# A graph network with two attentions on one core: the sixteen largest of a row of scores found through fourteen groups, and a new loop order

## Chip, core and metric

The program runs on one core of a Trainium2 chip. The metric is the device time of one execution in microseconds. Engines: PE (matmuls and transposes), DVE (vector engine), ACT (activations and copies), POOL (GpSimd), SP (issues the DMAs). Each engine works off its own instructions in order.

## The reference

Two rounds of a graph layer and an attention over 1250 nodes with 512 features. The change lies in the last part, the second attention, with 8 heads of 64 features. For every node and head it keeps the 16 largest of the 1250 scores and takes the softmax over these alone:

```python
logits = jnp.einsum('bmd,bpd->bmp', qd * scale, kd)
_, idx = lax.top_k(logits, TOPK)            # TOPK = 16
k_sel = gather(k, idx)
v_sel = gather(v, idx)
attn = jax.nn.softmax(jnp.einsum('bmd,bmkd->bmk', q * scale, k_sel), axis=-1)
out = jnp.einsum('bmk,bmkd->bmd', attn, v_sel)
...
return out @ wo_w.T + wo_b
```

The result is added to the features that went in.

## The kernel before

The nodes are cut into T = 10 tiles of P = 125 rows; the features into K = 4 pieces of 128. The stages run one after the other: adjacency counts, first graph layer, first attention, eight experts, second graph layer, projections, second attention. A general path for other inputs (`tile_general`) follows under a condition and runs only if the flag `bad` was set at the end.

The second attention is a hand-written order of instructions (`tc.manual_schedule`). It has 40 steps n; step n stands for the row tile i = n // 4 and a pair of heads j = n % 4; a_ = 0, 1 names the head of the pair. One turn of the loop mixes three steps: scores and selection of step n, transposes of step n - 1, products with the values of step n - 2. The helpers, with the engine that each keeps busy:

- `scores1` (PE, L1592): scores of one head in PSUM, a tile S of 3 x 512 columns of which 1250 are used, made in three chunks of two matmuls. There is one S for each a_, so the next scores of the same a_ wait until the last reader, the sign, is through.
- `first1` (DVE, L1606): the eight largest of the row; on POOL the negated maximum `nm` (L1607) and `gap` (L1608, L1609), a tiny distance that keeps the sixteenth itself inside the threshold.
- `without1` (DVE, L1617): a copy of the row, `rest`, in which these eight are replaced by a very low number.
- `second1` (DVE, L1626): the eight largest of `rest`; on POOL `below` (L1627), the negated threshold.
- `weights1` (ACT, L1634): e = exp(score - maximum) for all 1250 columns.
- `select1` (ACT, L1641): sg = sign(score + below), summed into `signs`; then on POOL e = e * sg (L1644). Columns outside the sixteen become negative.
- `turn1` (PE, L1654) and `keep1` (ACT, L1661): five groups of four transposes of e through one PSUM bank; ACT copies each group out with a Relu, which drops the negative columns. A group waits until the copy of the group before has emptied the bank.
- `values1` (PE, L1710) and `outputs1` (ACT, L1720): the product with the values. `project1` (PE, L1728) and `finish1` (DVE, L1736; DMA L1738): output projection, a quarter of the columns in each step, added to X and sent.
- `sums1`, `sums_exp1`, `sums_over1`, `sums_wide1`, `sums_turn1`, `sums_keep1`, `scale1`: once in four steps the sums of the sixteen weights of all heads, their inverses, and the scaling of the output (POOL L1670, L1684, L1698; ACT L1673, L1695; DVE L1677, L1678; PE L1691).
- `halves1`: in two of four steps the queries of the next row tile are split into a high and a low half (ACT L1577, POOL L1578) and copied to the other partitions by DMA (L1579, L1580).
- `signs_over1`, after the loop: if for any row the count in `signs` isn't that of sixteen columns, `bad` is set.

Lines used in the prediction from other stages: L644 (normalisation, DVE), L1383 (bias to X, POOL), L1530 (bias to X, DVE), L1091 (row maximum in the first attention, DVE, from PSUM), L776 (adjacency banks copied by ACT in transposed order, a stride of ten columns), L638 and L1421 (one-column operations on DVE).

Of the kernel before, what the change touches and what calls it, by code (L numbers as in the profile page):

```python
# [20 lines left out]
P = 125  # L21
# [551 lines left out]
def tile_usual(ctx: ExitStack, tc: tile.TileContext, a: dict, out: bass.AP):  # L573
# [969 lines left out]

    TINY = 2.0 ** -22
    wo_pool, wo_p = pool("wo", 1)
# [4 lines left out]
    with (  # L1550
# [6 lines left out]
        ps_s1 = (ps_s1a, ps_s1b)  # L1557
        w_v = at1.tile([128, K, D], F32, name="w_v1b", bufs=1)
# [4 lines left out]
        score, found, bests, es, pTs, outs, turned = {}, {}, {}, {}, {}, {}, {}  # L1563
# [18 lines left out]
        def scores1(n, a_, *chunks):  # L1582
# [6 lines left out]
            for c in chunks:  # L1589
                n0, n1 = c * 512, min(c * 512 + 512, N)  # L1590
                for x in range(2):
                    nc.tensor.matmul(score[n, a_][:, n0:n1], stacks[i][:, x, h, :], K2[:, h, n0:n1],  # L1592
                                     start=(x == 0), stop=(x == 1))


        def first1(n, a_):
            if n > last:
                return
# [5 lines left out]
            nm = at1.tile([P, 1], F32, tag=f"nm{a_}", name="nm1")  # L1604
            gap = at1.tile([P, 1], F32, tag=f"gap{a_}", name="gap")
            nc.vector.max(out=top[:, 0:8], in_=score[n, a_][:, :N])  # L1606
            nc.gpsimd.tensor_scalar(nm, top[:, 0:1], -1.0, None, op0=ALU.mult)  # L1607
            nc.gpsimd.tensor_scalar(gap, top[:, 7:8], -1.0, top[:, 0:1], op0=ALU.mult, op1=ALU.max)  # L1608
            nc.gpsimd.tensor_scalar(gap, gap, TINY, None, op0=ALU.mult)  # L1609
            found[n, a_] = (nm, gap, top)  # L1610

        def without1(n, a_):
            if n > last:
                return
            nm, gap, top = found[n, a_]
            rest = at1.tile([P, N], F32, name="rest", bufs=1)
            nc.vector.match_replace(out=rest, in_to_replace=top[:, 0:8], in_values=score[n, a_][:, :N],  # L1617
                                    imm_value=LOWEST)
            found[n, a_] = (nm, gap, top, rest)

        def second1(n, a_):
            if n > last:
                return
            nm, gap, top, rest = found[n, a_]
            below = at1.tile([P, 1], F32, tag=f"below{a_}", name="below")
            nc.vector.max(out=top[:, 8:16], in_=rest)  # L1626
            nc.gpsimd.tensor_scalar(below, top[:, 15:16], -1.0, gap, op0=ALU.mult, op1=ALU.add)  # L1627
            found[n, a_] = below

        def weights1(n, a_):  # L1630
# [3 lines left out]
            nc.scalar.activation(e, score[n, a_][:, :N], AF.Exp, bias=found[n, a_][0])  # L1634
            es[n, a_] = e

        def select1(n, a_):
# [3 lines left out]
            nc.scalar.activation(sg, score.pop((n, a_))[:, :N], AF.Sign, bias=found.pop((n, a_)),  # L1641
# [125 lines left out]
        with tc.manual_schedule():  # L1767
# [5 lines left out]
            for n in range(len(steps)):  # L1773


                i, c = n // K - 1, n % K
                if i >= 0 and c == 1:
                    sums_over1(i)
                first1(n, 0)
                values1(n - 2, 0, 5)  # L1780
                select1(n - 1, 1)
                turn1(n - 1, 0)
                values1(n - 2, 5, 8)
                keep1(n - 1, 0)
                without1(n, 0)
                if n == 1:
                    keep_late1()
                scores1(n, 1, 2, 1, 0)
                if n < 2:
                    values_late1(T - 3 + 2 * n)  # L1790
                if n <= last and c < 2:
                    halves1(steps[n][0] + 1, c)
                weights1(n, 0)
                turn1(n - 1, 1)
                values1(n - 2, 8, T)
                keep1(n - 1, 1)
                second1(n, 0)
                outputs1(n - 2)
                if i >= 0:
                    if c == 0:  # L1800
                        sums1(i)
# [139 lines left out]
```

## Time and profile before

| | us |
|---|---|
| median of three runs | 1541.5 (1539.97 to 1545.21) |
| the profiled execution | 1539.01 |
| its span, first to last instruction | 1537.1 |
| second attention within it (from 1106.8) | 430.3 |

In the second attention the engines are busy for: PE 383.1, DVE 369.4, ACT 336.0, POOL 319.1 us. Groups of instructions of this stage, each a line of the page's list of costliest groups:

| line, engine | what | count | mean ns |
|---|---|---|---|
| L1644 POOL | e * sg, 1250 columns | 79 | 2576 |
| L1641 ACT | sign, 1250 columns (and 208 to read the sum) | 80 | 1311 |
| L1634 ACT | exp, 1250 columns | 80 | 1302 |
| L1661 ACT | copy of four transposes | 200 | 590 |
| L1607, L1608, L1609, L1627 POOL | nm, gap, gap, below | 80 each | 215, 293, 213, 267 |
| L1578 POOL | low half of the queries | 18 | 1168 |
| L1698 POOL | scaling of the output | 9 | 1251 |

How to read them: the time of a group is that of the instructions alone; the idle time before it, and what ended that, stand behind it on the page. Instructions that don't need each other overlap a little at their ends, so the distance from start to start, read in the timeline, is shorter than the duration. The chain of waits goes back from the last instruction, at each step to what released it; its pieces show which wait ended last.

### The profile page before, as it was taken

How to read it: one execution, taken by the hardware profiler on the slowest of the kernel's cores; microseconds unless marked ns; L12 is line 12 of the kernel's file. 1: busy time of each engine (PE TensorE's matmuls, PEld its weight loads, DVE VectorE, ACT ScalarE, POOL GpSimd, SP SyncE). 2: the span in 40 equal slices, each digit the busy share in tenths (PEclk: the TensorE clock that was granted, in tenths of full speed). 3: DMA queues.
4: the chain of work that ended last, by engine and by line, in shares of the span. 5: the costliest groups of instructions: out<-in, count | busy, mean ns of one | idle time of the engine just before them, and what ended most of it. 6: DMA issues, size and time to landing. Idle time of an engine off the chain costs nothing.

```text
span 1537.1 us, 21430 instructions
## 1 busy us (share of the span) xinstructions
PE 1431.5 (93%) x8127; PEld 934.1 (61%) x8127; DVE 898.1 (58%) x1412; ACT 707.3 (46%) x1351; POOL 424.8 (28%) x621
## 2 busy tenths in 40 slices
PE   6999999978999998999999999989888999999997
PEld 4557744457778766444444446654466777777775
DVE  8895567544443332422222435653588998999894
ACT  3333444455555552210000223431278888888884
POOL 1110000011111120000000112210168787887873
PEclk9999999989999999999999999999999999999999
DMA  4001000010101010200001100000200000000000
GB/s 138 29 1 55 1 0 1 6 46 14 42 18 48 22 26 17 79 28 28 28 28 41 42 28 1 5 23 0 78 11 14 14 22 21 22 21 22 21 8 23
DMA packets 42323, 41.12 MB, mean 27 GB/s; under 512 B 25738, under 2 KB 30084, under 8 KB 42211
## 3 DMA queue, kind: packets, MB, share of 16 engines
q1 hardware_dynamic: 42211, 39.66, 8.9%
q8 instruction: 66, 1.08, 0.3%
q14 instruction: 46, 0.38, 0.1%
HBM read 26.81 MB, written 2.56 MB: 19 GB/s over the span
## 4 chain that ended last, share of the span: by engine, by line
PE 69%; DVE 13%; ACT 11%; issue 3%; POOL 2%; DMA 0%; ACTq 0%; SPq 0%; DVEq 0%; POOLq 0%
PE ps_o L1334 9%; PE ps_mm L1326 7%; PE S L1592 5%; PE ps_mm L865 5%; PE ps_t L1654 5%; PE ps_mm L800 5%; PE S L1034 4%; PE ps_mm L1462 4%; PE ps_o L870 4%; PE ps_t L1122 4%; PE O L1143 3%; PE O L1710 3%; ACT sg L1641 3%; PE bank L768 2%; PE O L1187 2%
## 5 line engine op out<-in xcount | busy, mean ns | idle before, releaser
L1644 POOL TENSOR_TENSOR e<-e,sg 125x1250 f32<-125x1250 f32 x79 | 203.5, 2576 | 35.0 <-ACT sg L1641 34.1
L1336 DVE SCALAR_TENSOR_TENSOR X<-ps_o,gate,X 125x512 f32<-125x512 f32 x80 | 60.0, 750 | 177.0 <-PE ps_o L1334 177.0
L1592 PE MATMUL S<-K,stacks 128*125 128x512 f32 (+1 forms) x480 | 123.9, 382 | 29.6 <-ACT sg L1641 25.4
L1654 PE MATMUL ps_t<-ident,e 125*125 125x125 f32 x800 | 132.3, 288 | 11.8 <-ACT R L1695 6.7
L1334 PE MATMUL ps_o<-we,hid 128*125 128x512 f32 x320 | 141.2, 595 | 0.0
L1661 ACT ACTIVATE pT<-ps_t 125x500 f32<-125x500 f32 x200 | 118.1, 590 | 50.1 <-PE ps_t L1654 49.2
L1606 DVE MAX8 best<-S 125x8 f32<-125x1250 f32 x80 | 117.0, 1462 | 32.9 <-PE S L1592 32.0
L1654 PEld LDWEIGHTS ps_t<-ident,e 125*125 125x125 f32 x800 | 105.6, 187 | 47.9 <-ACT pT L1661 27.4
L1329 ACT ACTIVATE hid<-ps_mm,b 128x500 f32<-128x500 f32 (+1 forms) x40 | 24.6, 615 | 209.0 <-PE ps_mm L1326 209.0
L1626 DVE MAX8 best<-rest 125x8 f32<-125x1250 f32 x80 | 117.1, 1464 | 2.7
L1617 DVE MATCH_REPLACE8 rest<-best,S 125x1250 f32<-125x1250 f32 x80 | 116.0, 1450 | 0.0
L1326 PE MATMUL ps_mm<-yT,we 128*128 128x500 f32 (+1 forms) x320 | 115.8, 520 | 0.0
L1641 ACT ACTIVATE sg<-S,below 125x1250 f16<-125x1250 f32 x80 | 104.9, 1311 | 17.5 <-POOL below L1627 17.5
L1710 PE MATMUL O<-pT,yT 125*64 125x125 f32 x1600 | 111.8, 277 | 0.0
L1592 PEld LDWEIGHTS S<-K,stacks 128*125 128x125 f32 x480 | 75.3, 190 | 51.0 <-ACT sg L1641 31.8
L1634 ACT ACTIVATE e<-S,nm 125x1250 f32<-125x1250 f32 x80 | 104.1, 1302 | 2.7 <-DVE rest L1617 1.6
L1334 PEld LDWEIGHTS ps_o<-we,hid 128*125 128x125 f32 x320 | 59.0, 187 | 72.4 <-issue 69.6
L1005 POOL TENSOR_TENSOR stacks<-yT,stacks 64x125 fp32r<-64x125 f32 x80 | 34.3, 428 | 232.1 <-ACT stacks L1004 228.7
L1127 ACT COPY pT<-ps_t 125x500 f32<-125x500 f32 (+3 forms) x112 | 54.8, 489 | 92.7 <-PE ps_t L1122 91.8
L1326 PEld LDWEIGHTS ps_mm<-yT,we 128*128 128x128 f32 x320 | 60.2, 189 | 55.2 <-issue 53.3
L1383 POOL TENSOR_TENSOR X<-X,beta 125x512 f32<-125x512 f32 x10 | 13.1, 1315 | 289.9 <-DVE h L644 289.9
L1710 PEld LDWEIGHTS O<-pT,yT 125*64 125x64 f32 x1600 | 83.8, 136 | 14.6 <-DVE bad L1764 0.8
(240 smaller groups left out, 2656.7 us busy)
## 6 DMA issues: line engine op xcount, KB each, us to landing
we<-in_W SPq DMA_DIRECT2D x16, 512.0 KB
stacks<-stacks SPq DMA_DIRECT2D x160, 31.2 KB
stacks<-stacks SPq DMA_DIRECT2D x40, 125.0 KB
X<-in_x SPq DMA_DIRECT2D x5, 500.0 KB
out<-y SPq DMA_DIRECT2D x10, 250.0 KB
w_n<-in_wn SPq DMA_DIRECT2D x1, 1024.0 KB
w_c<-in_wc SPq DMA_DIRECT2D x1, 1024.0 KB
w_q<-in_Wq SPq DMA_DIRECT2D x1, 1024.0 KB
```

Of the source, the lines that this page charges most:

```text
L1326: nc.tensor.matmul(ps[:, :n], w1[:, k, f * 128 : (f + 1) * 128], yT[:, k, span(t0, t1)], start=(k == 0), stop=(k == K - 1))
L1334: nc.tensor.matmul(ps[:P], hid[:, f, span(t, t + 1)], w2[:, f, :], start=(f == 0), stop=(f == FF // 128 - 1))
L1592: nc.tensor.matmul(score[n, a_][:, n0:n1], stacks[i][:, x, h, :], K2[:, h, n0:n1], start=(x == 0), stop=(x == 1))
L1606: nc.vector.max(out=top[:, 0:8], in_=score[n, a_][:, :N])
L1617: nc.vector.match_replace(out=rest, in_to_replace=top[:, 0:8], in_values=score[n, a_][:, :N], imm_value=LOWEST)
L1626: nc.vector.max(out=top[:, 8:16], in_=rest)
L1634: nc.scalar.activation(e, score[n, a_][:, :N], AF.Exp, bias=found[n, a_][0])
L1641: nc.scalar.activation(sg, score.pop((n, a_))[:, :N], AF.Sign, bias=found.pop((n, a_)), accum_out=signs[:, 2 * n + a_ : 2 * n + a_ + 1])
L1644: (nc.vector if 2 * n + a_ == 2 * last + 1 else nc.gpsimd).tensor_mul(e, e, sg)
L1654: nc.tensor.transpose(turned[n, g][:P, span(b - g0, b - g0 + 1)], es[n, b // T][:, span(b % T, b % T + 1)], ident[:P, :P])
L1661: nc.scalar.activation(pTs[n][:, g0:g1, :], turned.pop((n, g))[:P, : (g1 - g0) * P].rearrange("p (t n) -> p t n", n=P), AF.Relu)
L1710: nc.tensor.matmul(outs[n][a_ * DH : (a_ + 1) * DH, :P], V[:, t, h * DH : (h + 1) * DH], pT[:, a_ * T + t, :], start=(t == 0), stop=(t == ...
```

## The change

The two passes over the 1250 columns and the copy between them go. In their place `largest1` takes the eight largest of each of fourteen groups of columns (group k holds the columns k, k + 14, k + 28 and so on, 89 or 90 of them), directly from the scores in PSUM, into a tile of 14 x 8. `first1` and `second1` then find the eight largest and the next eight in these 112 numbers. `nm`, `gap` and `below` move from POOL to DVE; `gap` and `below` become one `scalar_tensor_tensor` each. If one group held more than eight of a row's sixteen, the count in `signs` would be off and `bad` set.

The loop's order is new: the value products stand together ahead of the scores, the score chunks are made in the order 1, 0, 2 for the second head and 2, 0, 1 for the first, the output's addition (`finish1`) stands between the maxima of the second head, and the pieces of the sums have other places. The tail behind the loop stays as it was.

```diff
--- before.py
+++ after.py
@@ -1541,7 +1541,10 @@
     TINY = 2.0 ** -22
+    SEARCHED = 14
     wo_pool, wo_p = pool("wo", 1)
     w_o = wo_p.tile([128, K, D], F32, name="w_o1")
     nc.sync.dma_start(w_o, a["wo"].rearrange("(k p) f -> p k f", p=128))
@@ -1555,12 +1558,13 @@
         tc.tile_pool(name="ps_s1a", bufs=1, space=PSUM) as ps_s1a,
     ):
         ps_s1 = (ps_s1a, ps_s1b)
+        PIECES = (((0, 512), (512, 1024), (1024, N)),) * 2
         w_v = at1.tile([128, K, D], F32, name="w_v1b", bufs=1)
         v_b = at1.tile([P, D], F32, name="v_b1b", bufs=1)
         signs = at1.tile([P, T * H], F32, name="signs", bufs=1)
         steps = [(i, j) for i in range(T) for j in range(K)]
         last = len(steps) - 1
-        score, found, bests, es, pTs, outs, turned = {}, {}, {}, {}, {}, {}, {}
+        score, largest, maxima, belows, bests, es, pTs, outs, turned = {}, {}, {}, {}, {}, {}, {}, {}, {}
@@ -1587,58 +1591,51 @@
             if (n, a_) not in score:
                 score[n, a_] = ps_s1[a_].tile([P, 3 * 512], F32, name="S")
             for c in chunks:
-                n0, n1 = c * 512, min(c * 512 + 512, N)
+                n0, n1 = PIECES[a_][c]
                 for x in range(2):
                     nc.tensor.matmul(score[n, a_][:, n0:n1], stacks[i][:, x, h, :], K2[:, h, n0:n1],
                                      start=(x == 0), stop=(x == 1))
+        def largest1(n, a_):
+            largest[n, a_] = at1.tile([P, SEARCHED, 8], F32, tag=f"largest{a_}", name="largest")
+            for k in range(SEARCHED):
+                nc.vector.max(out=largest[n, a_][:, k, :], in_=score[n, a_][:, k:N:SEARCHED])
         def first1(n, a_):
-            if n > last:
-                return
             i, j = steps[n]
             h = 2 * j + a_
             if h == 0:
                 bests[i] = at1.tile([P, H, TOPK], F32, name="best")
             top = bests[i][:, h, :]
-            nm = at1.tile([P, 1], F32, tag=f"nm{a_}", name="nm1")
+            nm = maxima[n, a_] = at1.tile([P, 1], F32, tag=f"nm{a_}", name="nm1")
+            nc.vector.max(out=top[:, 0:8], in_=largest[n, a_].rearrange("p g e -> p (g e)"))
+            nc.vector.tensor_scalar(nm, top[:, 0:1], -1.0, None, op0=ALU.mult)
+        def second1(n, a_):
+            i, j = steps[n]
+            top = bests[i][:, 2 * j + a_, :]
             gap = at1.tile([P, 1], F32, tag=f"gap{a_}", name="gap")
-            nc.vector.max(out=top[:, 0:8], in_=score[n, a_][:, :N])
-            nc.gpsimd.tensor_scalar(nm, top[:, 0:1], -1.0, None, op0=ALU.mult)
-            nc.gpsimd.tensor_scalar(gap, top[:, 7:8], -1.0, top[:, 0:1], op0=ALU.mult, op1=ALU.max)
-            nc.gpsimd.tensor_scalar(gap, gap, TINY, None, op0=ALU.mult)
-            found[n, a_] = (nm, gap, top)
-
-        def without1(n, a_):
-            if n > last:
-                return
-            nm, gap, top = found[n, a_]
-            rest = at1.tile([P, N], F32, name="rest", bufs=1)
-            nc.vector.match_replace(out=rest, in_to_replace=top[:, 0:8], in_values=score[n, a_][:, :N],
-                                    imm_value=LOWEST)
-            found[n, a_] = (nm, gap, top, rest)
-
-        def second1(n, a_):
-            if n > last:
-                return
-            nm, gap, top, rest = found[n, a_]
-            below = at1.tile([P, 1], F32, tag=f"below{a_}", name="below")
+            below = belows[n, a_] = at1.tile([P, 1], F32, tag=f"below{a_}", name="below")
+            rest = at1.tile([P, SEARCHED * 8], F32, name="rest")
+            nc.vector.match_replace(out=rest, in_to_replace=top[:, 0:8],
+                                    in_values=largest.pop((n, a_)).rearrange("p g e -> p (g e)"), imm_value=LOWEST)
+            nc.vector.scalar_tensor_tensor(gap, top[:, 7:8], -1.0, top[:, 0:1], op0=ALU.mult, op1=ALU.max)
             nc.vector.max(out=top[:, 8:16], in_=rest)
-            nc.gpsimd.tensor_scalar(below, top[:, 15:16], -1.0, gap, op0=ALU.mult, op1=ALU.add)
-            found[n, a_] = below
+            nc.vector.scalar_tensor_tensor(below, gap, TINY, top[:, 15:16], op0=ALU.mult, op1=ALU.subtract)
         def weights1(n, a_):
             if n > last:
                 return
             e = at1.tile([P, N], F32, tag=f"e{a_}", name="e")
-            nc.scalar.activation(e, score[n, a_][:, :N], AF.Exp, bias=found[n, a_][0])
+            nc.scalar.activation(e, score[n, a_][:, :N], AF.Exp, bias=maxima.pop((n, a_)))
             es[n, a_] = e
         def select1(n, a_):
             if not 0 <= n <= last:
                 return
             sg = at1.tile([P, N], F16, tag=f"sg{a_}", name="sg", bufs=1)
-            nc.scalar.activation(sg, score.pop((n, a_))[:, :N], AF.Sign, bias=found.pop((n, a_)),
+            nc.scalar.activation(sg, score.pop((n, a_))[:, :N], AF.Sign, bias=belows.pop((n, a_)),
                                  accum_out=signs[:, 2 * n + a_ : 2 * n + a_ + 1])
             e = es[n, a_]
             (nc.vector if 2 * n + a_ == 2 * last + 1 else nc.gpsimd).tensor_mul(e, e, sg)
@@ -1774,62 +1771,64 @@
                 i, c = n // K - 1, n % K
+                values1(n - 2, 0, 5)
+                if i >= 0 and c == 0:
+                    sums1(i)
+                largest1(n, 0)
+                turn1(n - 1, 0)
+                first1(n, 0)
+                if n == 1:
+                    keep_late1()
+                select1(n - 1, 1)
+                keep1(n - 1, 0)
+                values1(n - 2, 5, 8)
+                values1(n - 2, 8, T)
+                if c < 2:
+                    halves1(steps[n][0] + 1, c)
+                outputs1(n - 2)
+                if i >= 0 and c == 2:
+                    sums_turn1(i)
+                    sums_keep1(i)
+                scores1(n, 1, 1)
+                weights1(n, 0)
+                second1(n, 0)
+                scores1(n, 1, 0)
+                turn1(n - 1, 1)
+                scores1(n, 1, 2)
+                if n < 2:
+                    values_late1(T - 3 + 2 * n)
+                if i >= 0 and c == 3:
+                    scale1(i)
+                if i >= 1:
+                    project1(i - 1, c)
+                keep1(n - 1, 1)
                 if i >= 0 and c == 1:
                     sums_over1(i)
-                first1(n, 0)
-                values1(n - 2, 0, 5)
-                select1(n - 1, 1)
-                turn1(n - 1, 0)
-                values1(n - 2, 5, 8)
-                keep1(n - 1, 0)
-                without1(n, 0)
+                turn1(n - 1, 2)
+                largest1(n, 1)
+                select1(n, 0)
+                keep1(n - 1, 2)
+                finish1()
+                first1(n, 1)
+                if n == 0:
+                    keep_late1()
+                scores1(n + 1, 0, 2)
                 if n == 1:
                     keep_late1()
-                scores1(n, 1, 2, 1, 0)
-                if n < 2:
-                    values_late1(T - 3 + 2 * n)
-                if n <= last and c < 2:
-                    halves1(steps[n][0] + 1, c)
-                weights1(n, 0)
-                turn1(n - 1, 1)
-                values1(n - 2, 8, T)
-                keep1(n - 1, 1)
-                second1(n, 0)
-                outputs1(n - 2)
-                if i >= 0:
-                    if c == 0:
-                        sums1(i)
-                    if c == 1:
-                        sums_wide1(i)
-                    if c == 2:
-                        sums_turn1(i)
-                        sums_keep1(i)
-                    if c == 3:
-                        scale1(i)
-                first1(n, 1)
-                select1(n, 0)
-                turn1(n - 1, 2)
-                if i >= 1:
-                    project1(i - 1, c)
-                scores1(n + 1, 0, 2)
-                keep1(n - 1, 2)
+                turn1(n - 1, 3)
                 if i >= 0 and c == 0:
                     sums_exp1(i)
-                if n == 0:
-                    keep_late1()
-                without1(n, 1)
-                turn1(n - 1, 3)
                 keep1(n - 1, 3)
-                scores1(n + 1, 0, 0, 1)
+                scores1(n + 1, 0, 0)
+                weights1(n, 1)
+                scores1(n + 1, 0, 1)
                 if n == 0:
                     values_late1(T - 2)
-                weights1(n, 1)
                 turn1(n - 1, 4)
                 keep1(n - 1, 4)
                 second1(n, 1)
-                if n == 1:
-                    keep_late1()
-                finish1()
+                if i >= 0 and c == 1:
+                    sums_wide1(i)
```

## The prediction

> **What bounds the kernel now.** I read the page first, then the second attention stage in the chain of waits, the timeline and the groups by form. The page:
>
> ```profile
> span 1537.1 us, 21430 instructions
> ...
> PE 1431.5 (93%) x8127; PEld 934.1 (61%) x8127; DVE 898.1 (58%) x1412; ACT 707.3 (46%) x1351; POOL 424.8 (28%) x621
> ...
> L1606 DVE MAX8 best<-S 125x8 f32<-125x1250 f32 x80 | 117.0, 1462 | 32.9 <-PE S L1592 32.0
> ...
> L1626 DVE MAX8 best<-rest 125x8 f32<-125x1250 f32 x80 | 117.1, 1464 | 2.7
> ...
> L1617 DVE MATCH_REPLACE8 rest<-best,S 125x1250 f32<-125x1250 f32 x80 | 116.0, 1450 | 0.0
> ...
> L1641 ACT ACTIVATE sg<-S,below 125x1250 f16<-125x1250 f32 x80 | 104.9, 1311 | 17.5 <-POOL below L1627 17.5
> ```
>
> The shares of the whole span mislead: the change lies in one stage, from the first score matmul (1106.8 us) to the last sign (1513 us). In the busy time by window, its steady part is:
>
> ```profile
> core 0: us, PE busy (x) PEld busy (x) DVE busy (x) ACT busy (x) POOL busy (x), PEclk, DMA share, GB/s
> ...
> 1191.00:1231.00 40.00, 36.80 (x326) 29.74 (x325) 36.30 (x38) 33.50 (x53) 32.21 (x46) 1.00 0.06 14
> ```
>
> Four engines are nearly full, so the order of waits decides. The chain of waits through one step (two heads):
>
> ```profile
> 1201.78 0.27 issue
> 1202.05 0.59 ACT pT L1661
> 1202.64 1.29 ACT sg L1641 x2
> 1203.93 0.07 issue
> 1204.01 1.08 POOL e L1644
> ...
> 1207.84 0.28 POOL below L1627
> 1208.11 0.02 issue
> 1208.14 1.40 ACT sg L1641 x2
> 1209.54 0.04 issue
> 1209.58 0.47 PE S L1592 x2
> ```
>
> The sign of one head releases the multiply e*=sg on POOL; the small `below` of the other head is queued behind that multiply; the next sign waits for `below`, and only this sign frees the score buffer. A ring POOL-ACT-PE-DVE, then. Its period: in the same chain the first maximum of a block of four steps starts at 1191.20 and, seven blocks later, at 1472.92: 281.72/28 = 10.06 us per step.
>
> One thing more, from the stage before; the timeline shows a POOL and a DVE operation that meet:
>
> ```profile
> 885.67 1.27 POOL L1383 TENSOR_TENSOR X<-X,beta 125x512 f32<-125x512 f32 x1 [5.27 <-DVE h L644]
> 886.11 1.11 DVE L644 TENSOR_SCALAR h<-X,mv,rs 125x512 f32<-125x512 f32 x1
> ```
>
> and the list of one line's instructions (min/median/max) shows line 1530, which adds two SBUF tensors:
>
> ```profile
> L1530 DVE TENSOR_TENSOR X<-X,wo_b x8: 681/686/1719, 1076.5 to 1102.2; 125x512 f32<-125x512 f32 x8
> ```
>
> The operation of line 644, 0.55 us alone, ends 0.28 after POOL's end: it did its work only when POOL was through. Line 1530 takes 0.69 alone, 1.72 the one time POOL worked beside it. DVE's maxima, its match and the add of PSUM and SBUF (L1736, 268 to 272 ns) show no such thing, though POOL works beside most of them.
>
> **The change, part by part.** *Removed on DVE:* per head 1.48 + 1.54 + 1.48 = 4.5 us of whole passes. *Added:* fourteen maxima of 89 or 90 columns. The reductions of line 1091 take 283 ns at 125 columns and 1450 at 1250, 1.037 ns a column; so MAX8 at 90 is 1462 - 1160 x 1.037 = 260 ns, at 112 it is 280, the match at 112 is 270. Two independent maxima start 1.38 apart where one lasts 1.46 (1204.38 and 1205.76): 0.08 overlaps. Fourteen on end are 13 x 0.18 + 0.26 = 2.60 us; without overlap 14 x 0.26 = 3.64. I take 2.60, since that pair and the 0.27 us add (next start 0.19 later) both overlap. The stride of 14 in PSUM I cost at nothing: ACT's copies of line 776 read PSUM at a stride of ten and take 578 ns, the contiguous copy of equal size at line 1695 takes 576; DVE itself shows no strided read, and the upper end 3.64 has to cover one.
>
> [...]
>
> *After the fourteen*, per head: max of 112 (0.28), nm (0.15, from the one-column row of line 638), match (0.27 and its load 0.08), gap (0.16, the one-column row of line 1421), max (0.28), below (0.16). With 0.03 per hand-over, as between max and match now, DVE is held about 3.8 us a head, 7.9 a step with the small rest, against the 36.30/4 = 9.1 of the window above.
>
> *Moved from POOL to DVE:* nm, gap and below, 0.99 us a head. `below` no longer queues behind the multiply. But gap and below are now two-input operations, both inputs in SBUF, issued while POOL runs the multiply, which reads SBUF. The trace shows such a meeting at 512 columns only. Since the wait there ended with POOL's instruction, whatever DVE had left to do, I take it that a one-column operation waits too. Bounds: no wait, or until POOL's end plus 0 to 0.16; I take plus 0.06.
>
> [...]
>
> *The ring after:* sign to multiply 1.49 (1212.93 to 1214.42), multiply 2.57, gap 0.06, max 0.31, below 0.19: 4.62 from one head's sign to the other's. For the second head another path is longer. From the start of its maxima: 2.60 + 0.03, the max 0.31, the output add that now stands in front 0.19, nm 0.18, then on ACT e 1.19 and the fifth copy 0.47, both ahead of its sign: 4.97. And POOL's other work starts when the multiply ends, before `below` is issued: the low halves (1.07, two steps of four) hold it 1.07 - 0.37 = 0.70, the scaling (1.25, one of four) 0.88; (2 x 0.70 + 0.88)/4 = 0.57. Step: 4.62 + 4.97 + 0.57 = 10.16, against 10.06. Queued behind the waiting gap are below and the other head's fourteen maxima; behind below, the sign, the score buffer and the next matmuls.
>
> *At nothing:* the merged value products save PE a switch, but PE waits for the sign there anyway; score pieces in another order are complete at the same matmul count, and the maxima need all three; the halves' casts, subtractions and DMAs come two steps or more before their use (four transfers a block, 0.59 us each to issue on an SP queue that otherwise waits; late, they would hold the first scores of a block, one step in four, until they land); sums, exp and widening keep half a step or more of slack (without it, 0.3 to 0.6 us in one step of four). The start and the tail of the stage do not change.
>
> Sum: 39 steps x 0.10 = +4 us on the profiled execution (1537.1 in the span, 1539.0 in all), thus 1543. It was 2.5 us below the median of 1541.5, so I say **1545**.
>
> **Rivals.** *A: no wait at one column.* For it: all the waits seen are at 512 columns, and the one-column line 638 shows none. Against it: line 638 has one tensor, gap has two. Then ACT's queue rules: signs 2 x 1.27, e 2 x 1.19, copies 5 x 0.47, oT 0.15, casts, R and exp 0.42: 7.84; plus the one forced pause, third copy to transposes to fourth copy, 0.12 + 0.05 + 0.70 + 0.03 = 0.90, and some 0.2 round R: 8.94. 39 x 1.12 = 44 less: **1498**.
>
> *B: the short maxima do not overlap, or the stride costs as much (0.26 each).* For it: the trace has no chain of such short reads. Against it: the two pairs and line 776. DVE is then the bound: 7.9 + 2 x 1.04 = 9.98, plus 0.57 for below, plus 0.65 that gap still waits: 11.2. 39 x 1.14 = 44 more: **1586**. It decides as soon as a maximum costs more than 0.18: each 0.01 more lengthens the second path 0.14, 5.5 us in all.
>
> *C: the selection misses.* A row with more than eight of its sixteen in one group makes the check at the end start the general path, which does everything again: over 2500. Counted on the reference's own scores, no row of the 10,000 has more than eight in a group of stride 14, three have eight.
>
> **How the numbers follow.** Ring as worked out 0.56 (own range 1533 to 1558), A 0.20, B in part or whole 0.22, C and the unforeseen 0.02. 0.3%, 4.6 us, is what can be told from no change. The ring's case gives faster 0.12, same 0.18, slower 0.26; with A 0.20 faster and B and C 0.24 slower: 0.32, 0.18, 0.50. The range, 1493 to 1573, leaves out the outer half of B and the fringe of A.
>
> **What would show it.** The lines of gap and below tell most: means near 0.16 us are A; means of 0.5 to 1.2 with ends at POOL's ends are the ring. The fourteen should start 0.17 to 0.18 apart; 0.22 or more is B. In the ring POOL's multiply and ACT's sign alternate through the chain; in A the chain runs on ACT and PE, and a step takes 9.0. The prediction is wrong if gap never waits, or if DVE shows no pause at all.

## The result: 1547.9 us against 1541.5, and the profile after

The kernel after takes 1547.88 us in the median of 13 runs (1545.87 to 1548.83), the kernel before 1541.51 in 13 runs beside them (1539.65 to 1545.86): a ratio of 1.0039 with a 95% interval of 1.0031 to 1.0047. A search that kept DVE for 4.5 us a head was replaced by one that needs 3.2 (2.30 + 0.28 + 0.34 + 0.27, the timeline's durations), and the time grew by 6 us. From the page after, the lines that answer to those shown of before:

```profile
span 1545.8 us, 22441 instructions
...
PE 1426.6 (92%) x8127; PEld 939.7 (61%) x8127; DVE 922.8 (60%) x2772; ACT 706.1 (46%) x1351; POOL 350.1 (23%) x301
...
PE 61%; DVE 27%; ACT 8%; issue 2%; DMA 1%; POOL 0%; DVEq 0%; ACTq 0%; SPq 0%
...
L1603 DVE MAX8 largest<-S 125x8 f32<-125x89 f32 (+1 forms) x1120 | 183.3, 238 | 3.9 <-PE S L1596 3.6
...
L1638 ACT ACTIVATE sg<-S,below 125x1250 f16<-125x1250 f32 x80 | 104.6, 1308 | 22.6 <-DVE below L1625 22.3
...
L1623 DVE SCALAR_TENSOR_TENSOR gap<-best 125x1 f32<-125x1 f32 x80 | 101.3, 1267 | 0.0
```

POOL works 75 us less than before. DVE, which lost 350 us of whole passes (117.0 + 116.0 + 117.1), is nonetheless busier, 922.8 against 898.1. The fourteen maxima take 183 of it; and a new name is among the costliest: `gap`, an operation on one number per partition, at 1.27 us each. The sign now waits 22 us for DVE's `below`, where it waited 17.5 for POOL's.

The busy time of the same forty microseconds as before (PE, weight loads, DVE, ACT, POOL, then granted clock, DMA):

```profile
1191.00:1231.00 40.00, 35.43 (x324) 29.64 (x324) 38.30 (x174) 33.25 (x53) 24.85 (x13) 1.00 0.07 14
```

DVE 38.3 of 40: by this row, and by the chain of waits, DVE is now the bound:

```profile
1208.25 1.32 DVE gap L1623
1209.57 0.20 DVE best L1624
...
1209.86 0.87 DVE below L1625
```

Much of this busy time is waiting, as e1 below shows, and this is the trap of this profile. The timeline of the same place, with POOL beside it, shows what the 1.4 and the 0.9 us are:

```profile
1206.98 2.57 POOL L1641 TENSOR_TENSOR e<-e,sg 125x1250 f32<-125x1250 f32 x1 [2.23 <-ACT sg L1638]
...
1207.85 0.15 DVE L1613 TENSOR_SCALAR nm<-best 125x1 f32<-125x1 f32 x1
...
1208.17 1.40 DVE L1623 SCALAR_TENSOR_TENSOR gap<-best 125x1 f32<-125x1 f32 x1
...
1209.63 1.07 POOL L1582 TENSOR_TENSOR stacks<-qT,stacks 64x500 fp32r<-64x500 f32 x1
...
1209.86 0.86 DVE L1625 SCALAR_TENSOR_TENSOR below<-gap,best 125x1 f32<-125x1 f32 x1
```

`gap` ends at 1209.57, POOL's multiply at 1209.55; `below` ends at 1210.72, POOL's low halves at 1210.70, and the sign, with ACT idle for 0.71 us, starts at 1210.82. `nm`, in the middle of the multiply, takes its 0.15. The lists of the three lines (min/median/max in ns):

```profile
L1613 DVE TENSOR_SCALAR nm<-best x80: 153/154/157, 1116.6 to 1515.9; 125x1 f32<-125x1 f32 x80
```
```profile
L1623 DVE SCALAR_TENSOR_TENSOR gap<-best x80: 150/1210/2468, 1116.9 to 1516.2; 125x1 f32<-125x1 f32 x80
```
```profile
L1625 DVE SCALAR_TENSOR_TENSOR below<-gap,best x80: 159/328/1105, 1117.4 to 1517.6; 125x1 f32<-125x1 f32 x80
```

Over the whole stage, 79 of 80 gaps began inside a POOL operation, and every one of these ended 0.00 to 0.03 us after that operation's end; so did 45 of 80 `below`; the other 35 took 0.16. At 0.16 of real work each, 80 x 1.11 + 80 x 0.29 = 112 us of DVE's "busy" time in the stage (391.7) is standing still.

To compare kernels in the steady part, the starts of the signs in the timeline are used, over 32 steps. Distance to the first head's sign of a step, by the step's place c = n % 4 in the row tile, then the mean distance from the first to the second head's sign, then the step. The last column is the step at full clock: the mean over the four places c of those steps in which the granted TensorE clock stays at 1.00, without the last of the 32, which no low halves follow (us; the runs are those of the next section):

| | c=0 | c=1 | c=2 | c=3 | second head | step | at full clock |
|---|---|---|---|---|---|---|---|
| before | 5.34 | 5.71 | 5.46 | 4.42 | 4.80 | 10.03 | 10.06 |
| after | 5.20 | 5.41 | 5.11 | 5.37 | 4.87 | 10.15 | 10.08 |
| gap alone with two tensors (e5) | 4.68 | 4.69 | 5.03 | 4.69 | 4.87 | 9.64 | 9.56 |
| below alone with two tensors (e6) | 4.36 | 4.50 | 5.03 | 4.36 | 4.80 | 9.36 | 9.36 |
| neither (e1) | 4.36 | 4.50 | 5.03 | 4.37 | 4.80 | 9.36 | 9.36 |

After against before, the 32 steps together take 3.6 us more (0.11 a step), but 2.8 of this lies in two steps alone: they take 11.49 and 11.36 us where the others of the same c take 10.19 and 9.82. In each of the two the granted clock stands at half for 3.4 us. The busy time by window shows it, with the 3.4 us ahead of each:

```profile
1157.60:1161.00 3.40, 1.49 (x11) 1.05 (x9) 3.30 (x16) 2.72 (x6) 1.82 (x3) 1.00 0.33 70
1161.00:1164.40 3.40, 3.40 (x13) 2.88 (x12) 2.79 (x12) 2.05 (x4) 2.24 (x1) 0.50 0.03 6
1290.70:1294.10 3.40, 1.83 (x15) 1.46 (x14) 3.37 (x18) 1.89 (x4) 1.76 (x2) 1.00 0.19 38
1294.10:1297.50 3.40, 3.40 (x18) 2.79 (x18) 3.33 (x18) 2.44 (x4) 2.17 (x2) 0.50 0.00 0
```

PE was busy for 1.49 and 1.83 of the 3.40 us, then its clock was halved. The kernel before has no such stretch in these steps. At full clock a step grew by 0.01 to 0.02 us, less than 1 us in 39.

The whole stage, from its first score matmul to the end, grew by 4.1 us, from 430.3 to 434.4: 2.9 less up to the sign of step 4, 3.6 more in the 32 steps, 3.4 more behind them. The rest of the profiled difference, 4.6 us, lies ahead of that matmul (it starts at 1111.5 instead of 1106.9), in code that didn't change; other profiled kernels of this study start it between 1108.7 and 1111.3, so that part is probably mostly the scatter of runs.

### The profile page after: what moved, and what is told of

Its sections match the earlier page's. It is cut to its first block, busy times and chain, and to the rows that moved or that the text cites. A ratio compares the mean times of both kernels' runs of the same rounds, so it can differ in the third digit from the quotient of the medians.

```text
span 1545.8 us, 22441 instructions
## 1 busy us (share of the span) xinstructions
PE 1426.6 (92%) x8127; PEld 939.7 (61%) x8127; DVE 922.8 (60%) x2772; ACT 706.1 (46%) x1351; POOL 350.1 (23%) x301
## 3 DMA queue, kind: packets, MB, share of 16 engines
q8 instruction: 66, 1.08, 0.3%
## 4 chain that ended last, share of the span: by engine, by line
PE 61%; DVE 27%; ACT 8%; issue 2%; DMA 1%; POOL 0%; DVEq 0%; ACTq 0%; SPq 0%
PE ps_o L1334 9%; DVE largest L1603 8%; PE ps_mm L1326 7%; PE ps_mm L865 5%; PE ps_mm L800 5%; DVE gap L1623 4%; PE S L1034 4%; PE ps_mm L1462 4%; PE ps_o L870 4%; PE ps_t L1122 4%; PE O L1143 3%; PE bank L768 2%; PE O L1187 2%; DVE below L1625 2%; PE S L1596 2%
## 5 line engine op out<-in xcount | busy, mean ns | idle before, releaser
L1641 POOL TENSOR_TENSOR e<-e,sg 125x1250 f32<-125x1250 f32 x79 | 203.3, 2573 | 161.8 <-ACT sg L1638 147.2
L1603 DVE MAX8 largest<-S 125x8 f32<-125x89 f32 (+1 forms) x1120 | 183.3, 238 | 3.9 <-PE S L1596 3.6
L1596 PE MATMUL S<-K,stacks 128*125 128x512 f32 (+1 forms) x480 | 134.7, 391 | 49.0 <-ACT sg L1638 43.8
L1651 PE MATMUL ps_t<-ident,e 125*125 125x125 f32 x800 | 132.1, 288 | 6.9 <-ACT pT L1658 6.2
L1596 PEld LDWEIGHTS S<-K,stacks 128*125 128x125 f32 x480 | 79.5, 192 | 70.8 <-ACT sg L1638 51.6
L1707 PE MATMUL O<-pT,yT 125*64 125x125 f32 x1600 | 105.5, 278 | 0.0
L1623 DVE SCALAR_TENSOR_TENSOR gap<-best 125x1 f32<-125x1 f32 x80 | 101.3, 1267 | 0.0
L1034 PE MATMUL S<-K,stacks 128*125 128x512 f32 (+10 forms) x288 | 84.4, 401 | 7.1 <-ACT e L1101 6.6
L1122 PE MATMUL ps_t<-ident,e 125*125 125x125 f32 x440 | 81.7, 296 | 9.5 <-ACT pT L1127 6.0
```

What stands on the lines that cost most here:

```text
L1034: nc.tensor.matmul(ps[:, n0:w], stacks[n][:, x, a_, :], K2[:, 2 * j + a_, n0:w], start=(x == 0), stop=(x == 1))
L1122: nc.tensor.transpose(ps[:P, span(t - t0, t - t0 + 1)], es[n, a_][:, span(t, t + 1)], ident[:P, :P])
L1603: nc.vector.max(out=largest[n, a_][:, k, :], in_=score[n, a_][:, k:N:SEARCHED])
L1623: nc.vector.scalar_tensor_tensor(gap, top[:, 7:8], -1.0, top[:, 0:1], op0=ALU.mult, op1=ALU.max)
L1641: (nc.vector if 2 * n + a_ == 2 * last + 1 else nc.gpsimd).tensor_mul(e, e, sg)
L1651: nc.tensor.transpose(turned[n, g][:P, span(b - g0, b - g0 + 1)], es[n, b // T][:, span(b % T, b % T + 1)], ident[:P, :P])
```

## The experiments

Ten kernels. Ratios are to the kernel before, run beside them. The step is the mean over the same 32 steps as above, stretches at half clock included.

| run | median us | ratio (95%) | step us |
|---|---|---|---|
| e1 both lines with pointer operands | 1517.2 | 0.983 (0.981 to 0.986) | 9.36 |
| e2 gap and below on POOL | 1576.5 | 1.022 (1.019 to 1.025) | 11.01 |
| e3 old search, new order | 1757.7 | 1.139 (1.136 to 1.142) | 15.54 |
| e4 new search, old order | 1524.3 | 0.989 (0.986 to 0.991) | 9.54 |
| e5 only gap with two tensors | 1527.9 | 0.991 (0.989 to 0.993) | 9.64 |
| e6 only below with two tensors | 1518.0 | 0.984 (0.983 to 0.986) | 9.36 |
| e7 both pointers, two pieces moved | 1511.3 | 0.981 (0.979 to 0.983) | 9.24 |
| e8 only nm with two tensors | 1601.7 | 1.039 (1.037 to 1.041) | 11.58 |
| e9 as e7, two copies to DVE | 1509.0 | 0.978 (0.977 to 0.980) | 9.17 |
| e10 old search, old order, small operations on DVE | 1550.2 | 1.005 (1.003 to 1.008) | 10.22 |

### e1: the wait taken away

```diff
-            nc.vector.scalar_tensor_tensor(gap, top[:, 7:8], -1.0, top[:, 0:1], op0=ALU.mult, op1=ALU.max)
+            nc.vector.tensor_scalar(gap, top[:, 7:8], -1.0, top[:, 0:1], op0=ALU.mult, op1=ALU.max)
...
-            nc.vector.scalar_tensor_tensor(below, gap, TINY, top[:, 15:16], op0=ALU.mult, op1=ALU.subtract)
+            nc.vector.tensor_scalar(below, gap, TINY, top[:, 15:16], op0=ALU.mult, op1=ALU.subtract)
```

> Everything as after the change, but gap and below read their second column as a per-partition pointer operand of a tensor_scalar (L1623, L1625), so each has one tensor input instead of two. Theory (the ring: a DVE operation with two tensor inputs in SBUF stands still until POOL's multiply is through): both now take 0.15 to 0.17 us, DVE loses its pauses, ACT's queue rules, a step takes about 9.0 us instead of 10.1, the time is 1495 to 1510 us. Rival 1 (the new order or ACT sets the step, the long gap only fills a pause that would be there anyway): gap and below short, but 1543 to 1550 us. Rival 2 (a pointer operand waits for POOL just as a tensor does): gap stays at 1.2 us and the time at 1547 us.

1517.22 us, 31 less than after, by one word in each of two lines. The list of gap's line:

```profile
L1623 DVE TENSOR_SCALAR gap<-best x80: 201/204/207, 1115.9 to 1487.4; 125x1 f32<-125x1 f32 x80
```

No wait is left; `below` takes 212 to 216 ns. The pointer form costs 0.05 us more than the 0.15 to 0.17 expected and does not wait for POOL. Rivals 1 and 2 fall. At full clock the step fell from 10.08 to 9.36, 39 x 0.72 = 28 of the 31 us. DVE's busy time in the stage fell by 97 us (391.7 to 294.7) and the time by 31: so much of the standing had been off the path. But 1517 misses the 1495 to 1510 of the theory too. The chain of one plain step says why:

```profile
1222.59 1.40 ACT sg L1638 x2
...
1226.59 1.23 PE O L1707 x20
1227.81 0.63 PE ps_t L1651 x4
1228.44 1.22 PE O L1707 x20
1229.66 1.12 PE S L1596 x4
1230.78 0.45 PE ps_t L1651 x4
1231.28 0.46 issue
1231.74 1.40 ACT sg L1638 x2
```

From one sign to the same head's next are 9.15 us, and from the end of the first, 1224.0, to 1231.2 PE works without a pause. The value products, the scores of the other head and the transposes stand in one queue between the sign and the copy that the next sign stands behind. ACT's own queue, 8.94 in the prediction, was not the longest.

### e5 and e6: one line at a time

e5 (a plain two-tensor operation for gap, so the kind of operation is another too; the sign of gap is turned, and `below` multiplies by -TINY):

```diff
-            nc.vector.tensor_scalar(gap, top[:, 7:8], -1.0, top[:, 0:1], op0=ALU.mult, op1=ALU.max)
+            nc.vector.tensor_tensor(gap, top[:, 7:8], maxima[n, a_], ALU.min)
```

> Of the two lines only gap has two tensor inputs, and as a plain tensor_tensor (the smaller of the eighth value and nm); below stays in the pointer form. Theory (two tensor inputs in SBUF wait for POOL's end, whatever the operation): gap stays at 1.1 to 1.3 us in the mean though the operation is another, below takes 0.21, and what is won against the kernel after is what below waited there for POOL's small pieces, (449 - 214) ns x 80 = 19 us if all of it lay on the path: 1525 to 1535 us. Rival (it is the operation scalar_tensor_tensor that waits): gap short, 1515 to 1520 us.

e6, against e1:

```diff
-            nc.vector.tensor_scalar(below, gap, TINY, top[:, 15:16], op0=ALU.mult, op1=ALU.subtract)
+            nc.vector.scalar_tensor_tensor(below, gap, TINY, top[:, 15:16], op0=ALU.mult, op1=ALU.subtract)
```

> The other half: gap in the pointer form, below as the scalar_tensor_tensor of the change. Theory: the wait moves to below, which starts some 0.5 us later and ends at the same end of POOL's multiply; below takes 0.7 to 1.0 us in the mean, gap 0.20; the sign then comes 0.5 us earlier than in the kernel after, since the last maximum is no longer behind the wait, and POOL's next piece cannot slip in ahead: 1517 to 1528 us. Rival (every such operation costs about the same, so each half is worth half): 1530 to 1535 us.

The list of gap in e5, then that of `below` in e6:

```profile
L1623 DVE TENSOR_TENSOR gap<-best,nm x80: 151/1323/2418, 1115.6 to 1497.6; 125x1 f32<-125x1 f32 x80
```
```profile
L1625 DVE SCALAR_TENSOR_TENSOR below<-gap,best x80: 160/1030/2045, 1116.3 to 1487.9; 125x1 f32<-125x1 f32 x80
```

Both kinds of operation tried wait when they have two tensor inputs in SBUF; again the waits end 0.00 to 0.03 us after POOL. 1527.9 and 1518.0 us, both as the theory had them (the mean of `below` in e6, 1.08 us, lies a little above its 0.7 to 1.0). Between them they split the 31 us: when only gap waits, the step costs 0.28 us more than e1 (0.20 at full clock), 10.6 us in all; when `below` can in addition meet POOL's next piece, another 20.0 us. And when `below` alone waits, 0.92 us longer than needed on average, 73 us of DVE's time, it costs nothing that can be told (1518.0 against 1517.2): it then meets only the multiply (79 of 79) and ends with it, before the sign is due anyway, and no longer starts so late that it meets POOL's next piece.

### e8: a line that never waited

```diff
-            nc.vector.tensor_scalar(nm, top[:, 0:1], -1.0, None, op0=ALU.mult)
+            nc.vector.scalar_tensor_tensor(nm, top[:, 0:1], -2.0, top[:, 0:1], op0=ALU.mult, op1=ALU.add)
```

> Gap and below in the pointer form, but nm, which has one tensor input and never waited in any run so far, is written with two (-2 x maximum + maximum, the same number). Theory: nm now stands until POOL's end, 1.2 to 1.7 us in the mean, gap and below are short; match, maximum and below come after the wait, so the ring is 1.49 + 2.57 + 0.06 + 0.27 + 0.08 + 0.20 + 0.31 + 0.21 = 5.2 us a head and e is late as well: 10.3 to 11 us a step, 1550 to 1585 us. Rival (the waits of gap and below came from where these stand, not from their two inputs): nm 0.15 us, 1515 to 1520 us.

```profile
L1613 DVE SCALAR_TENSOR_TENSOR nm<-best x80: 159/2246/2566, 1115.4 to 1570.1; 125x1 f32<-125x1 f32 x80
```

The list of nm: 2.25 us in the median, and gap and below short. The form of the operands makes the wait, not the place. The time, 1601.7, is above what was expected: the exp and a copy of transposes stand on ACT behind nm and ahead of the sign. Sign to multiply 1.47, multiply 2.57, nm's end 0.02 after it, then 1.70 over exp and copy to the sign: 5.76, as measured (5.71 to 5.83 a head). The expectation had followed DVE's queue only.

### e2: back on POOL

```diff
-            nc.vector.scalar_tensor_tensor(gap, top[:, 7:8], -1.0, top[:, 0:1], op0=ALU.mult, op1=ALU.max)
+            nc.gpsimd.tensor_scalar(gap, top[:, 7:8], -1.0, top[:, 0:1], op0=ALU.mult, op1=ALU.max)
+            nc.gpsimd.tensor_scalar(gap, gap, TINY, None, op0=ALU.mult)
...
-            nc.vector.scalar_tensor_tensor(below, gap, TINY, top[:, 15:16], op0=ALU.mult, op1=ALU.subtract)
+            nc.gpsimd.tensor_scalar(below, top[:, 15:16], -1.0, gap, op0=ALU.mult, op1=ALU.add)
```

> As after the change, but gap (two instructions) and below go back to POOL as before it; nm stays on DVE. Theory (ring): DVE no longer waits for POOL, but below is queued behind the multiply again, so the ring through POOL, ACT and PE stays closed: 1.49 + 2.57 + 0.28 + 0.05 = 4.4 us from one head's sign to the other's, 4.97 for the second head's path at most, POOL's small pieces behind the multiply in some steps: 9.6 to 9.9 us a step, 1525 to 1540 us. Rival (only the DVE pause costs, queueing behind the multiply does not): about 9.0 us a step, 1495 to 1510 us.

A miss: 1576.5 us. From its timeline:

```profile
1205.90 2.57 POOL L1642 TENSOR_TENSOR e<-e,sg 125x1250 f32<-125x1250 f32 x1 [1.51 <-ACT sg L1639]
...
1208.45 0.30 POOL L1623 TENSOR_SCALAR gap<-best 125x1 f32<-125x1 f32 x1
...
1208.84 0.21 POOL L1624 TENSOR_SCALAR gap<-gap 125x1 f32<-125x1 f32 x1
1209.15 0.26 POOL L1626 TENSOR_SCALAR below<-best,gap 125x1 f32<-125x1 f32 x1
```

In the old search 3 us of DVE passes lay between gap and below, so gap ran before the multiply. With the short search all three are behind it: 0.97 us instead of the 0.33 expected, 5.02 from sign to sign (1204.42 to 1209.44 in the same timeline), and 6.30 where the low halves stand between as well. In this order the operations had to leave POOL for the short search to be worth anything; as the change moved them, they took the wait for POOL along in another form. The short search with these operations on POOL in the old order was not run.

### e3, e4, e10: search and order apart

All three have the small operations on DVE in the pointer form. e4 is e1 with the loop of before. e10 is the kernel before with nm, gap and below as in e1. e3 has the loop of after with the old three passes:

```diff
+            nc.vector.max(out=bests[i][:, h, 0:8], in_=score[n, a_][:, :N])
...
+            rest = at1.tile([P, N], F32, name="rest", bufs=1)
+            nc.vector.match_replace(out=rest, in_to_replace=top[:, 0:8], in_values=score[n, a_][:, :N],
+                                    imm_value=LOWEST)
```

> The new loop order with the old search: maximum, replacement and second maximum over all 1250 columns, the small operations on DVE with pointer operands, so that none has two tensor inputs. Tells the order from the search. Theory: the three whole passes keep DVE for 4.5 us a head and the small rest some 0.5, 9.6 to 10.0 us a step with the output's add, DVE is the bound and the order alone wins nothing: 1520 to 1550 us. Rival (the order is what could win, and the search is only along for the ride): 9.0 to 9.3 us a step, 1495 to 1510 us.

> The new search, gap and below with pointer operands, in the loop order from before the change. Theory: with the search short and without the pause behind POOL, the order matters little: 9.0 to 9.3 us a step, 1495 to 1515 us. Rival (the search pays only in the new order, since in the old one the second head's search starts too late or a score buffer comes free too late): 1520 to 1545 us.

> The kernel before, with nothing changed but nm, gap and below, which go from POOL to DVE in the pointer form: old search and old order. With the runs of the new search in both orders and of the old search in the new order this makes the four cases complete. Theory (the old search keeps DVE as the next bound as soon as below no longer queues on POOL): DVE needs per step 6 x 1.46 - 4 x 0.08 + 2 x (0.15 + 0.20 + 0.21) + 0.3 = 9.9 us, so 1535 to 1543 us: the small operations alone win nearly nothing. Rival (POOL's queue was all that bound it, the shorter search is not needed): 1515 to 1528 us.

| small operations on DVE, no wait | old order | new order |
|---|---|---|
| old search | 1550.2 (e10) | 1757.7 (e3) |
| new search | 1524.3 (e4) | 1517.2 (e1) |

The short search is worth 26 us in the old order; the new order is worth 7 more, and only with the short search. e4 lies 9 us above its theory's range, at the lower end of its rival's; the theory had a step of 9.0 to 9.3 in it, and like that of e1 it was too short (9.54; 9.49 at full clock). The rival's reason, that the search pays only in the new order, does not hold at 17 us below the kernel before. e10 is 7 us over its range, with DVE in its chain as expected:

```profile
1210.67 1.39 DVE best L1606
1212.08 0.15 DVE nm L1607
1212.23 0.12 DVE gap L1608
1212.35 1.45 DVE rest L1616
...
1213.82 1.47 DVE best L1625
```

So moving the small operations alone makes the kernel slower; only with the short search is there room on DVE. e3 missed by 200 us. Its timeline:

```profile
1207.40 1.31 ACT L1629 ACTIVATE e<-S,nm 125x1250 f32<-125x1250 f32 x1
...
1208.82 1.45 DVE L1619 MATCH_REPLACE8 rest<-best,S 125x1250 f32<-125x1250 f32 x1
...
1212.12 1.30 ACT L1636 ACTIVATE sg<-S,below 125x1250 f16<-125x1250 f32 x1 [2.93 <-DVE below L1623]
```

The replacement waits for the exp of the same scores (80 times, 224 us in all by its list), although it needs nothing from it: in the new order the exp is written first. In the kernel before it is the other way round, and there the exp waits for the replacement (three times, 10.8 us by the list of its line). So in these kernels two engines' reads of one S follow each other as they are written; whether the chip asks for that or only the program's own waits was not tried. With the short search the second pass reads SBUF, not S, and has nothing to wait for there.

### e7 and e9: what is left

e7 is e1 with the output copy behind the exp, and the second group of transposes ahead of a chunk of scores:

```diff
-                outputs1(n - 2)
...
                 weights1(n, 0)
+                outputs1(n - 2)
                 second1(n, 0)
-                scores1(n, 1, 0)
                 turn1(n - 1, 1)
-                scores1(n, 1, 2)
+                scores1(n, 1, 0, 2)
```

> Both lines in the pointer form, and two pieces moved: the output copy on ACT (L1717) behind the exp of the first head instead of ahead of it, and the second group of transposes (turn1) ahead of the second head's chunk 0 of scores. In the run with both pointers ACT stands 0.45 us ahead of that copy in a step, waiting for PE's value products, and the sign behind it sets when PE can go on. Theory: the sign of the first head comes 0.3 to 0.4 us earlier in most steps, 1502 to 1512 us. Rival (PE is full and the pause moves elsewhere): 1514 to 1520 us.

e9 takes e7 and gives two copies to DVE, written behind `second1(n, 0)`:

```diff
-            nc.scalar.copy(R, turned.pop(i)[:, : K * P].rearrange("p (k n) -> p k n", k=K))
+            nc.vector.tensor_copy(R, turned.pop(i)[:, : K * P].rearrange("p (k n) -> p k n", k=K))
...
-            nc.scalar.copy(oTs[i][:, j, :], outs.pop(n)[:, :P])
+            nc.vector.tensor_copy(oTs[i][:, j, :], outs.pop(n)[:, :P])
```

> The better order, and two copies out of PSUM go from ACT to DVE: the output copy (L1717, 0.26 us a step) and the copy of the turned inverses (L1692, 0.58 us in one step of four), both behind the second maximum of the first head. Each has one tensor input, so neither should wait for POOL. Theory: ACT, which lies on the path between the transposes and the sign, loses 0.26 + 0.58/4 = 0.4 us a step, and about 0.1 to 0.3 of it shows: 9.0 to 9.15 us a step, 1500 to 1508 us. Rival (PE sets the step now): 1509 to 1514 us.

1511.3 and 1509.0 us. e7 came into its range, at the upper end: against e1 the first head's sign comes 0.31, 0.13 and 0.47 us earlier at c = 0, 1 and 3, but 0.16 later at c = 2. e9 ends one microsecond above its theory's range and at its rival's edge; the intervals of the two overlap, so it isn't shown to be faster than e7. Its chain from 1200 to 1230 us, by line:

```profile
by line: PE ps_t L1651 26.0%; PE O L1707 24.5%; PE S L1596 22.2%; PE O L1725 7.0%; ACT pT L1658 5.9%; ACT sg L1638 4.3%; ACT e L1631 3.0%; DVE R L1692 2.3%; issue 2.1%; ACT stacks L1581 2.0%; PE ps_t L1688 2.0%; DVEq L1692 0.1%
```

PE's own matmuls and transposes are 82% of it. With the two-tensor forms gone, two pieces moved and two copies given to DVE, the change that had cost 6 us beats the kernel before by 32 (ratio 0.9783, 0.9765 to 0.9801).

## Why the prediction was right, step by step

The wait on which the prediction was built is there, and taking it away wins 31 us. The rise of 0.10 us a step, from which the sum was made, is not there at full clock: that the number still came out within 3 us is in part luck.

- **The ring: its first part right, the rise of the step not.** Worked out were 4.62 us from the second head's sign to the next first head's, 4.97 for the second head and 0.57 of holding, 10.16 a step against 10.06. Over the 32 steps 10.15 was measured, at full clock 10.08 against 10.06. The timeline above gives the pieces of the 4.62: sign to multiply 1.48, multiply 2.57, gap's end 0.02 after it, 0.29 to below; below alone takes 0.16, and from its end to the sign are 0.10. In that step the low halves hold it longer; e5, where only this part is left, measures 4.68 at c = 0, 1 and 3 at full clock (its below takes 0.05 longer). But the first head came to 5.27 for 5.19, and the second to 4.81 for 4.97: a difference of 0.10 between two steps of 10 us was smaller than the errors of its terms.
- **A one-column operation waits like a wide one: right, and shown both ways**, by taking the wait away (e1) and by giving it to a line that had none (e8). Taken was POOL's end plus 0.06 within 0 to 0.16; it is 0.00 to 0.03, with one element per partition: gap takes 1.27 us in the mean of after, 0.15 the one time that it began beside no POOL operation. Line 644, one of the two rows from which this was concluded, is however no two-tensor operation: it has one tensor and two pointers, at 512 columns.
- **POOL's other work holds below: right, its parts less so.** Counted were the low halves at 0.70 and the scaling at 0.88. Against e5, both at full clock, they cost 0.60 and 0.72 (c = 0 and 1) and 0.69 (c = 3). Left out were the inverses' turn and copy at c = 2: 5.03 with no wait at all, in e1 as well. In the kernel before, c = 3 had been the short step (4.42), since below stood in POOL's queue ahead of the scaling; now POOL begins the scaling when the multiply ends. That one place takes back what the other three win.
- **Second head's path: near in size, but another path.** 4.97 came from fourteen maxima of 2.60; with what they take, 2.30, the path is 4.67. But 4.80 stands there in before, e1 and e6 alike, and 4.81 in after at full clock (the 4.87 of the table holds the two steps at half clock): in e1's chain it is the sign, a score chunk, transposes, their copy, the exp and another copy.
- **Fourteen maxima: mis-sized, 2.60 for 2.30.** They start 0.16 apart, not 0.18. A stride of fourteen is not seen in the time: one takes 0.24, where 0.26 had been worked out without it. Rival B fell with this. DVE's hold of 3.8 us a head in it is not what its listed terms add to (3.98 with no hand-over); in e1, without waits, DVE is busy for 7.2 us a step, not 7.9.
- **Rival A: not the case, and mis-sized.** With the waits gone it forecast 8.94 a step and 1498; e1 has 9.36 and 1517.2. ACT's queue had been added up, PE's, between the sign and its next, had not.
- **What would show it: one sign was wrong.** The lines of gap and below told it as said, with means (1.27 and 0.45) just outside the 0.5 to 1.2. But POOL's multiply does not alternate with the sign in the chain: it has 0% of it, since a wait inside an instruction looks like that instruction's work.
- **The sum: near, by other terms.** +4 us on the profiled stage was forecast and 4.1 measured, but 39 steps at full clock give less than 1. The two stretches at half clock give 2.8; they were not in the prediction. The start and the tail, put at no change, gave 2.9 less and 3.4 more; in that tail the clock stands at half for 6.8 us from 1516.0, in the kernel before not until 1533.2, and how much of the 3.4 this makes is not shown. The executions on record point the same way: the kernel before took 1539.9 to 1540.1 us at a granted clock of 0.991 over the whole run, 1543.8 to 1545.3 at 0.987 and 1545.9 at 0.985; the kernel after stood at 0.985 in eleven of 13, at 1546.6 to 1548.8. At like clocks the two lie some 2 us apart or less, not 6.

## What to carry to other kernels

When work moves from POOL to DVE so as not to queue behind a long POOL instruction, look at its operands: with two tensor inputs in SBUF the one-column operations here waited for that instruction all the same (gap 1.27 us in the mean of after, 0.15 alone), and DVE's whole queue with them. In an operation on one column the second operand can be passed as a per-partition pointer instead (0.20 us for gap in e1, with no wait); for wider ones this is not shown (see below). And an instruction whose minimum and median differ eightfold at one shape (gap in after, 150 and 1210 ns) is probably waiting, whatever the busy time and the chain say: compare its end with the ends on the other engine, and then ask what stands behind it, since here the same wait cost 31 us, 11 us or nothing according to what followed.

## What the runs showed of the hardware

- At one column a pointer operand is no second input in this sense: the 160 of e1 took 0.20 to 0.22 us, 156 of them begun while POOL was at work. Wider operations with pointers can wait all the same: line 644, with one tensor and two pointers at 512 columns, takes 0.55 us alone and took 1.11 to 1.12 the three times that it began inside a POOL operation, in before and after alike. What tells the two apart was not tried. The add of X and O (L1733), one input from SBUF and one from PSUM, takes 0.27 beside POOL's multiply.
- POOL, which was at work first in all these meetings, does not pay for them: its multiply takes 2573 ns in after and 2574 in e1.
- The granted TensorE clock sank where PE stood idle for more of the time. From 1150 us to near the end of the stage:

| | e1 | before | after | e2 | e8 | e3 |
|---|---|---|---|---|---|---|
| granted clock | 1.00 | 1.00 | 0.99 | 0.95 | 0.94 | 0.83 |
| PE idle, share | 6% | 9% | 13% | 16% | 18% | 30% |
| PE's longest wait, us | 0.8 | 2.2 | 1.6 | 2.6 | 2.0 | 3.6 |
| score matmul, mean ns | 383 | 377 | 387 | 403 | 414 | 481 |

The longest wait does not order these kernels; the idle share does. In before and after the clock stands at half for 3.41, 6.83 or 10.24 us at a time, but for the last stretch of each, which reaches to the end. Ahead of a fall PE worked little: in the twelve traces the clock falls to half 140 times, and in the 3.41 us before that PE was busy for at most 0.63 of the time, for at most 0.55 in 126 of them; of the 5059 other stretches of that length at full clock, counted back from each fall, 16 lie at 0.55 or below. Before and after alone have 14 falls, with 0.61 at most and 0.54 at most in 13 of them, and 3 of their 857 other stretches lie at 0.55 or below. No run was made to test whether this is what brings the clock down. How much of what e2, e3 and e8 lost is slower matmuls, beyond their waits, was not taken apart.
